# Two changes to a graph-network kernel: the dilation's compare goes from VectorE to GpSimd, and the layers' last batches are handled in smaller steps

## The chip, the cores and the metric

The kernel runs on one core of a Trainium2 chip. The metric is the device time of one execution in microseconds (us). A core has five engines that run their own instructions in order and wait for each other by semaphores: TensorE (in the profile PE, its weight loads PEld), VectorE (DVE), ScalarE (ACT), GpSimd (POOL) and SyncE (SP, which here only starts transfers).

## The reference, cut to what matters

There are B = 16 graphs of N = 1024 nodes with D = 128 features, and a dense weight matrix `adj` per graph. Two blocks follow each other.

Block 0 (`layer0` in the kernel) runs three times

```python
h = h @ W + b
nh = h / max(norm(h), EPS)
h = (adj * (nh @ nh.T)) @ h
```

on the normalised input and adds the result to `x`.

Block 1 first thins the adjacency out ("dilation"). Row by row, each row's present neighbours are counted; `rank` is the running count along the row, and every neighbour whose rank is a multiple of half the count (rounded up) is removed, with its mirror image, before the next row is looked at. With more than ten neighbours this removes the neighbour at half of the count, and the last one if the count is even. Rows with ten or fewer neighbours lose all. Then come three "sage" layers:

```python
out = (adj_d @ x / deg) @ Wr + x @ Wx + b
out = out / max(norm(out), NORM_EPS) * mask
h = batchnorm(relu(out))          # mean and variance over all 16 graphs
```

and the output is `concat(h1, h2, h3) @ Wl + bl`, masked and added to `x`. Because the batch norm needs the statistics of all sixteen graphs, a sage layer can't begin before the layer in front of it has ended for the last graph.

## The kernel before, in words

A graph is called a batch, P = 128, NCH = 8 chunks of 128 nodes, CPH = 4 chunks make a half. The program is written with a tile framework: the code gives the dataflow and its order, the framework's scheduler places each engine's instructions in an order of its own (with the code's order as the priority) and adds the semaphores. A tile's `tag` and `bufs` say how many copies of it exist; a new one has to wait until the last user of the oldest copy is done.

**Layer 0 and the dilation, together.** `layer0()` is a generator of units of TensorE work. Each block row of a batch takes a product of the normalised features (`pg`, L344), a multiplication with `adj` on VectorE (`ew`, L353 and L356), transposes (`gt`, L373) with a copy on ScalarE (L374), and sums (`po`, L384 and L398). `hS` (L321, GpSimd) holds the normalised features of a batch; the adjacency's transposed blocks are stored from GpSimd's queue (L262). `dilation()` is a second generator. The main loop takes a piece of the dilation, then as many units of layer 0 as a fixed share of estimated work allows, and so on, so that the two advance together.

The dilation goes over 16 blocks: eight row blocks `k` of 128 rows, each in two halves of BH = 8 batches. A block has three parts.

- `loads`: fetches `adj`, turns it into a 0/1 pattern (L587, L588) and multiplies the part left of the diagonal with what earlier row blocks kept (`kl`, read back from DRAM by a transposing transfer, and `patt`, L594).
- `rounds`: settles within the block which neighbours go, by iterating small steps between VectorE (`E` at L667 and a dozen operations on single columns) and TensorE (L673). It leaves `radius` and `shift`, so that a neighbour is to be removed exactly where |shift - rank| equals radius.
- `scans`: for each batch a running sum over 1024 columns on VectorE (`rank`, L740, three buffers), the absolute value of its distance from the shift on ScalarE (L749, in place), a comparison with the radius (`kp`, L760 on VectorE, two buffers), and a store of the result to DRAM from GpSimd's queue (`keep`, L761).

The comparison in question is

```python
nc.vector.tensor_scalar(kp, rank, radius[:, i : i + 1], None, ALU.not_equal)
nc.gpsimd.dma_start(keep_d[b][cols, :], kp)
```

A second form of the dilation (`exact=True`) stands in a branch that is taken only if the first found a row that it can't treat; with these inputs it doesn't run.

**The sage layers.** Per batch, `weighted` makes `hw` and `own` (`pw`, L860 to L862), `Sums.add` accumulates 64 blocks in PSUM (`agg`, L888), `weigh` divides by the degree and adds (`o`, L917). `norms(h)`, per half, squares four chunks on ScalarE (L933), takes the inverse root in three small steps (`ss`, `rn`, L154 to L157), multiplies with the mask (L937) and scales four chunks at once on GpSimd (L938). `keep(h)` transposes the half (`pt_r`, L165), applies relu on ScalarE into `hR` (L166) and takes statistics (L948). After the last batch `batchnorm` combines all statistics (L953 to L961) into a factor and an offset per feature. `normed` applies them to a batch with one ScalarE instruction (L1052).

In the second and third sage layer `start2(l, b)` is called while batch b - 1 is at its third block row. It normalises batch b's features of the layer before, begins its sums, and projects those same features with `wl` (`pp`, L1062) into `acc`: a copy for the first layer's features, an addition for the second's. In the third layer `residual(b)` multiplies `acc` with the squared mask and adds `x`. After the third layer a last loop over the batches normalises, projects and adds into `y`, which is stored.

Of the kernel before, what the change touches and what calls it, by code (L numbers as in the profile page):

```python
# [12 lines left out]
ALU = mybir.AluOpType  # L13
# [33 lines left out]
def tile_adj_preln_d2(  # L47
# [152 lines left out]
    with ExitStack() as actx:  # L200
# [362 lines left out]
        def dilate(k, half, exact):  # L563
# [161 lines left out]
            def scans():  # L725
# [9 lines left out]
                for i in range(BH + 1):  # L735
# [18 lines left out]
                    if exact:  # L754
                        nc.vector.tensor_scalar(
                            kp, rank, low[:, i : i + 1], radius[:, i : i + 1], ALU.max, ALU.not_equal
                        )
                        nc.vector.tensor_tensor(kp, kp, pt[:, 2:], ALU.is_ge)
                    else:
                        nc.vector.tensor_scalar(kp, rank, radius[:, i : i + 1], None, ALU.not_equal)  # L760
# [76 lines left out]
    with ExitStack() as bctx:  # L837
# [29 lines left out]
        class Sums:  # L867
# [58 lines left out]
            def norms(self, h):  # L926
# [4 lines left out]
                for c in range(CPH):  # L931
                    n = h * CPH + c
                    nc.scalar.activation(  # L933
                        self.own[:, n, :], self.o[:, n, :], AF.Square, accum_out=ss[:, c : c + 1]
                    )
                rn = inv_root(pool2, ss, nm)
                nc.vector.tensor_tensor(rn, rn, mf[:, b, hc], ALU.mult)  # L937
                nc.gpsimd.tensor_tensor(  # L938
                    self.o[:, hc, :], self.o[:, hc, :], rn.unsqueeze(2).to_broadcast([P, CPH, D]), ALU.mult
                )  # L940
# [24 lines left out]
        with kctx, ExitStack() as c1:  # L965
# [42 lines left out]
            def follow():  # L1008
                nonlocal last
                s, q, aT = behind.pop(0)  # L1010
                s.add(q, aT)
                if q == CPH + 1:
                    s.norms(0)
                if q == NCH - 1:
                    s.norms(1)
                    last = s
# [33 lines left out]
        def normed(l, b, ab):  # L1050
            hT = pool2.tile([P, NCH, P], F32, tag="hT2", name=f"hT2_{l}_{b}")
            nc.scalar.activation(  # L1052
                hT.rearrange("p c q -> p (c q)"), hR[:, b, :], AF.Identity, bias=ab[:, 1:2], scale=ab[:, 0:1]
            )
# [9 lines left out]

        def start2(l, b):
            hT = normed(l, b, ab)
            got = Sums(l, b, hT, CPH, 0, ps_a)
            for h, pp, a in project(l - 1, b, hT):
                if l == 1:
                    nc.scalar.activation(a, pp, AF.Copy)  # L1070
                else:
                    nc.vector.tensor_tensor(a, pp, a, ALU.add)
            return got
# [12 lines left out]
        for l in (1, 2):  # L1086
            last = None
            then = start2(l, 0)
            for b in range(B):
                now = then  # L1090
# [17 lines left out]
                now.norms(1)  # L1108
                last = now
            last.keep(1)  # L1110
            ab = batchnorm(l)

# [68 lines left out]
```

## Time and profile before

| | us |
|---|---|
| median of 3 runs | 2877.07 (2874.56 to 2882.93) |
| the profiled execution's own time | 2874.98 |
| its span in the profile | 2873.2 |
| TensorE busy | 2659.3 (93%) |
| VectorE busy | 1939.7 (68%) |
| ScalarE busy | 1426.0 (50%) |
| GpSimd busy | 473.7 (16%) |

The comparisons of L760 lie between 86.9 and 1565.8 us of the span, layer 0 ends near 1692, and the three sage layers end near 2150, 2490 and 2829 us. In the profile a group of instructions is given as line, engine, operation, output <- inputs by the program's names, shapes and count, then busy time in us and mean of one in ns, then the idle time of its engine just before them and what ended most of it. "x128" is a count. PEclk is TensorE's granted clock as a share of the full one. Matmuls are pipelined, so a busy TensorE isn't a TensorE at its peak. In a timeline the number in brackets is the engine's idle time before the instruction, in us.

### The profile page before, as it was taken

How to read it: one execution, taken by the hardware profiler on the slowest of the kernel's cores; microseconds unless marked ns; L12 is line 12 of the kernel's file. 1: busy time of each engine (PE TensorE's matmuls, PEld its weight loads, DVE VectorE, ACT ScalarE, POOL GpSimd, SP SyncE). 2: the span in 40 equal slices, each digit the busy share in tenths (PEclk: the TensorE clock that was granted, in tenths of full speed). 3: DMA queues.
4: the chain of work that ended last, by engine and by line, in shares of the span. 5: the costliest groups of instructions: out<-in, count | busy, mean ns of one | idle time of the engine just before them, and what ended most of it. 6: DMA issues, size and time to landing. Idle time of an engine off the chain costs nothing. (4 is left out here: it accounts for less than half of the span.)

```text
span 2873.2 us, 51953 instructions
## 1 busy us (share of the span) xinstructions
PE 2659.3 (93%) x18803; PEld 2199.0 (77%) x18803; DVE 1939.7 (68%) x4913; ACT 1426.0 (50%) x4100; POOL 473.7 (16%) x619
## 2 busy tenths in 40 slices
PE   6999998999999998989998998999989999899997
PEld 4666666666666666666676778898879999899996
DVE  3778778778878778789877467677762333356565
ACT  6767557557556556556455333333333433333334
POOL 3112112112011111112111012222220010010102
PEclk9999999999999999999999999999999999999998
DMA  9447247248366476286253249999985665577764
GB/s 287 130 139 236 77 155 236 86 137 247 87 186 178 99 199 191 80 257 191 55 190 115 75 168 380 379 401 401 397 333 191 202 213 202 183 236 229 237 230 134
DMA packets 382233, 585.22 MB, mean 204 GB/s; under 512 B 85200, under 2 KB 266448, under 8 KB 381968
## 3 DMA queue, kind: packets, MB, share of 16 engines
q1 hardware_dynamic: 343280, 425.28, 47.2%
q0 software_dynamic: 38688, 156.53, 14.5%
q8 instruction: 151, 2.47, 0.4%
q14 instruction: 114, 0.93, 0.1%
HBM read 403.44 MB, written 163.58 MB: 197 GB/s over the span
## 5 line engine op out<-in xcount | busy, mean ns | idle before, releaser
L888 PE MATMUL agg<-hw,aT 128*128 128x128 f32 (+1 forms) x6144 | 744.4, 277 | 8.2 <-DVE aT L985 7.3
L888 PEld LDWEIGHTS agg<-hw,aT 128*128 128x128 f32 x6144 | 713.6, 193 | 13.4 <-DVE aT L985 9.7
L344 PE MATMUL pg<-nhT 128*128 128x512 f32 (+3 forms) x1152 | 460.2, 502 | 69.5 <-DVE ew L356 65.5
L384 PE MATMUL po<-ew,hS 128*128 128x512 f32 (+3 forms) x1152 | 458.4, 501 | 8.7 <-ACT hTo L407 5.4
L356 DVE TENSOR_TENSOR ew<-pg,adjA 128x768 f32<-128x768 f32 (+3 forms) x528 | 423.2, 825 | 5.8 <-PE pg L344 5.7
L398 PEld LDWEIGHTS po<-ew,hS 128*128 128x128 f32 x2688 | 338.4, 193 | 40.3 <-issue 37.8
L398 PE MATMUL po<-ew,hS 128*128 128x128 f32 x2688 | 365.3, 277 | 1.2 <-ACT ew L374 1.2
L374 ACT ACTIVATE ew<-gt 128x512 f32<-128x512 f32 (+1 forms) x480 | 209.2, 465 | 247.8 <-PE gt L373 237.6
L344 PEld LDWEIGHTS pg<-nhT 128*128 128x128 f32 x1152 | 189.0, 194 | 164.8 <-issue 120.9
L740 DVE TENSOR_TENSOR_SCAN rank<-patt 128x1024 f16<-128x1024 f16 x128 | 295.0, 2316 | 0.9
L384 PEld LDWEIGHTS po<-ew,hS 128*128 128x128 f32 x1152 | 197.9, 195 | 100.8 <-issue 66.4
L373 PEld LDWEIGHTS gt<-ident,ew 128*128 128x128 f32 x1344 | 168.3, 143 | 100.2 <-issue 72.1
L353 DVE TENSOR_TENSOR ew<-pg,adjA 128x128 f32<-128x128 f32 x384 | 107.6, 280 | 184.9 <-PE pg L344 142.8
L938 POOL TENSOR_TENSOR o<-o,rn 128x512 f32<-128x512 f32 x96 | 111.4, 1160 | 646.6 <-DVE rn L937 627.7
L373 PE MATMUL gt<-ident,ew 128*128 128x128 f32 x1344 | 212.7, 276 | 4.9 <-PEq L822 2.4
L860 PE MATMUL pw<-wrx,hT 128*128 128x256 f32 x768 | 179.5, 388 | 10.5 <-ACT hT L1052 9.7
L862 DVE TENSOR_TENSOR own<-pw,bs 128x256 f32<-128x256 f32 x192 | 81.3, 424 | 156.9 <-ACT hw L861 156.8
L860 PEld LDWEIGHTS pw<-wrx,hT 128*128 128x128 f32 x768 | 145.0, 194 | 32.6 <-ACT hT L1052 10.5
L933 ACT ACTIVATE own<-o 128x128 f32<-128x128 f32 x384 | 114.4, 300 | 104.1 <-DVE o L917 104.0
L1003 ACT ACTIVATE aT<-pta 128x512 f32<-128x512 f32 (+3 forms) x160 | 71.1, 466 | 187.7 <-PE pta L1002 164.2
L749 ACT ACTIVATE rank<-rank,fin 128x1024 f16<-128x1024 f16 x128 | 146.7, 1151 | 30.8 <-DVE rank L740 30.2
L321 POOL TENSOR_TENSOR hS<-hN,rn 128x1024 f32<-128x1024 f32 x48 | 97.2, 2025 | 372.4 <-DVE rn L157 265.9
(165 smaller groups left out, 3910.5 us busy)
## 6 DMA issues: line engine op xcount, KB each, us to landing
an<-in_adj_dram SPq DMA_DIRECT2D x128, 512.0 KB, 4.4
keep<-kp POOLq DMA_DIRECT2D x128, 256.0 KB, 2.9
kb<-keep SPq DMA_DIRECT2D x128, 256.0 KB, 5.6
aT<-adT SPq DMA_DIRECT2D x32, 960.0 KB, 4.7
aT<-adT SPq DMA_DIRECT2D x32, 832.0 KB, 4.6
aT<-adT SPq DMA_DIRECT2D x32, 704.0 KB, 4.2
aT<-adT SPq DMA_DIRECT2D x32, 576.0 KB, 3.4
xb<-in_x_dram SPq DMA_DIRECT2D x31, 512.0 KB, 4.9
```

The lines of the kernel that those rows point to most:

```text
L344: nc.tensor.matmul(pg[:, :n, :].rearrange("p c q -> p (c q)"), lhsT=self.nhT[:, q * P : (q + 1) * P], rhs=self.nhT[:, (q + c) * P : (q + c ...
L356: nc.vector.tensor_tensor(both[0][:, :, off, :], pg[:, own:n, :].unsqueeze(1).to_broadcast([P, 2, n - own, P]), both[1][:, :, off, :], ALU ...
L373: nc.tensor.transpose(pt[:, i, :], ew[:, at + i, :], ident)
L374: nc.scalar.activation(ew[:, at : at + n, :], pt[:, :n, :], AF.Copy)
L384: nc.tensor.matmul(self.po[:, c * P : (c + n) * P], lhsT=self.hS[:, q, :], rhs=ew[:, c - q : c - q + n, :].rearrange("p c q -> p (c q)"), ...
L398: nc.tensor.matmul(self.po[:, q * P : (q + 1) * P], lhsT=self.hS[:, q + n, :], rhs=ew[:, NCH - 1 - q + n, :], start=False, stop=closes and ...
L740: nc.vector.tensor_tensor_scan(rank, pt[:, 1 : N + 1], pt[:, 2:], 0.0, ALU.add, ALU.add)
L749: nc.scalar.activation(rank, rank, AF.Abs, bias=shift[:, i : i + 1], scale=1.0 if exact else -1.0)
L860: nc.tensor.matmul(pw[:, i, :], lhsT=hT[:, 2 * h + i, :], rhs=wrx[:, l, :], start=True, stop=True)
L888: nc.tensor.matmul(self.place(c), lhsT=aT[:, blk, :], rhs=self.hw[:, source, :], start=source == 0 and c % self.ga == 0, stop=ends(c, source),
L933: nc.scalar.activation(self.own[:, n, :], self.o[:, n, :], AF.Square, accum_out=ss[:, c : c + 1])
L938: nc.gpsimd.tensor_tensor(self.o[:, hc, :], self.o[:, hc, :], rn.unsqueeze(2).to_broadcast([P, CPH, D]), ALU.mult)
```

## The change

There are four edits.

1. In the dilation, the comparison goes from VectorE to GpSimd, as one instruction with two steps (equal to the radius, then less than 0.5, which is 1 where it was not equal). The store follows it on GpSimd's queue as before.
2. `norms` has a form `soon`, used for the second half of each sage layer's last batch: two of four squares on VectorE, and the scaling as four instructions on VectorE instead of one on GpSimd.
3. `normed` treats batch 0 in four instructions of two chunks instead of one of eight.
4. In the second and third sage layer, the last batch's projection is taken out of `start2` and put between that batch's sums and its `keep(1)`. Its results are added to `acc` after `batchnorm` in the code; in the third layer, where `residual` has already scaled `acc`, they are multiplied with the squared mask on the way.

```diff
@@ -757,7 +757,8 @@
                         )
                         nc.vector.tensor_tensor(kp, kp, pt[:, 2:], ALU.is_ge)
                     else:
-                        nc.vector.tensor_scalar(kp, rank, radius[:, i : i + 1], None, ALU.not_equal)
+
+                        nc.gpsimd.tensor_scalar(kp, rank, radius[:, i : i + 1], 0.5, ALU.is_equal, ALU.is_lt)
                     nc.gpsimd.dma_start(keep_d[b][cols, :], kp)
                     yield False, 0.8
 
@@ -923,21 +924,29 @@
                         ALU.add,
                     )
 
-            def norms(self, h):
+            def norms(self, h, soon=False):
 
                 nm, b = f"{self.l}_{self.b}_{h}", self.b
                 hc = slice(h * CPH, (h + 1) * CPH)
                 ss = pool2.tile([P, CPH], F32, tag="in_ss", name=f"ss_{nm}")
                 for c in range(CPH):
-                    n = h * CPH + c
-                    nc.scalar.activation(
-                        self.own[:, n, :], self.o[:, n, :], AF.Square, accum_out=ss[:, c : c + 1]
-                    )
+                    o, sq = self.o[:, h * CPH + c, :], self.own[:, h * CPH + c, :]
+                    if soon and c >= CPH // 2:
+                        nc.vector.scalar_tensor_tensor(
+                            sq, o, 1.0, o, ALU.mult, ALU.mult, accum_out=ss[:, c : c + 1]
+                        )
+                    else:
+                        nc.scalar.activation(sq, o, AF.Square, accum_out=ss[:, c : c + 1])
                 rn = inv_root(pool2, ss, nm)
                 nc.vector.tensor_tensor(rn, rn, mf[:, b, hc], ALU.mult)
-                nc.gpsimd.tensor_tensor(
-                    self.o[:, hc, :], self.o[:, hc, :], rn.unsqueeze(2).to_broadcast([P, CPH, D]), ALU.mult
-                )
+                if soon:
+                    for c in range(CPH):
+                        o = self.o[:, h * CPH + c, :]
+                        nc.vector.tensor_scalar(o, o, rn[:, c : c + 1], None, ALU.mult)
+                else:
+                    nc.gpsimd.tensor_tensor(
+                        self.o[:, hc, :], self.o[:, hc, :], rn.unsqueeze(2).to_broadcast([P, CPH, D]), ALU.mult
+                    )
 
             def keep(self, h):
 
@@ -1012,7 +1021,7 @@
                 if q == CPH + 1:
                     s.norms(0)
                 if q == NCH - 1:
-                    s.norms(1)
+                    s.norms(1, soon=s.b == B - 1)
                     last = s
 
             then = ahead1
@@ -1049,9 +1058,16 @@
 
         def normed(l, b, ab):
             hT = pool2.tile([P, NCH, P], F32, tag="hT2", name=f"hT2_{l}_{b}")
-            nc.scalar.activation(
-                hT.rearrange("p c q -> p (c q)"), hR[:, b, :], AF.Identity, bias=ab[:, 1:2], scale=ab[:, 0:1]
-            )
+
+            n = NCH if b else 2
+            for c in range(0, NCH, n):
+                nc.scalar.activation(
+                    hT[:, c : c + n, :].rearrange("p c q -> p (c q)"),
+                    hR[:, b, c * P : (c + n) * P],
+                    AF.Identity,
+                    bias=ab[:, 1:2],
+                    scale=ab[:, 0:1],
+                )
             return hT
 
         def project(l, b, hT):
@@ -1062,15 +1078,22 @@
                     nc.tensor.matmul(pp[:, c, :], lhsT=hT[:, h * CPH + c, :], rhs=wl[:, l, :], start=True, stop=True)
                 yield h, pp, acc[:, b, h * CPH : (h + 1) * CPH, :]
 
+        def taken(l, pp, a):
+
+            if l == 0:
+                nc.scalar.activation(a, pp, AF.Copy)
+            else:
+                nc.vector.tensor_tensor(a, pp, a, ALU.add)
+
         def start2(l, b):
+
             hT = normed(l, b, ab)
             got = Sums(l, b, hT, CPH, 0, ps_a)
+            if b == B - 1:
+                return got, hT
             for h, pp, a in project(l - 1, b, hT):
-                if l == 1:
-                    nc.scalar.activation(a, pp, AF.Copy)
-                else:
-                    nc.vector.tensor_tensor(a, pp, a, ALU.add)
-            return got
+                taken(l - 1, pp, a)
+            return got, None
 
         def residual(b):
 
@@ -1087,7 +1110,7 @@
             last = None
             then = start2(l, 0)
             for b in range(B):
-                now = then
+                now, hT = then
                 for q in range(NCH):
                     aT = row_of(q, f"{l + 1}_{b}")
                     nc.sync.dma_start(aT, adT_d[b][q])
@@ -1105,10 +1128,22 @@
                         now.norms(0)
                     if q == NCH - 2 and b == B - 1:
                         now.keep(0)
-                now.norms(1)
+                now.norms(1, soon=b == B - 1)
                 last = now
+
+            late = list(project(l - 1, B - 1, hT))
             last.keep(1)
             ab = batchnorm(l)
+            for h, pp, a in late:
+                if l == 1:
+                    taken(0, pp, a)
+                    continue
+
+                for c in range(CPH):
+                    n = h * CPH + c
+                    nc.vector.scalar_tensor_tensor(
+                        a[:, c, :], pp[:, c, :], mf2[:, B - 1, n : n + 1], a[:, c, :], ALU.mult, ALU.add
+                    )
 
         for b in range(B):
             y = pool2.tile([P, NCH, D], F32, tag=("o", "own")[b % 2], name=f"y_{b}")
```

## The prediction

> **What bounds the kernel.** First the page's busy times, then a table of stages, then the waits of TensorE (PE) and VectorE (DVE) in the first stage, then the durations of the instructions concerned, last the timeline around a layer's end.
>
> ```profile
> PE 2659.3 (93%) x18803; PEld 2199.0 (77%) x18803; DVE 1939.7 (68%) x4913; ACT 1426.0 (50%) x4100; POOL 473.7 (16%) x619
> ```
>
> PE is busy nearly all the time; GpSimd (POOL) is nearly idle. The stages (stretch, then busy time with instruction count for each engine, granted PE clock, DMA share, GB/s):
>
> ```profile
> 100.00:1570.00 1470.00, 1356.03 (x8539) 989.68 (x8537) 1172.07 (x2782) 878.20 (x2350) 242.24 (x309) 0.99 0.52 155
> 1570.00:1692.00 122.00, 118.79 (x687) 86.67 (x685) 56.05 (x141) 38.13 (x114) 8.44 (x6) 1.00 0.19 64
> ...
> 2142.00:2156.00 14.00, 7.68 (x22) 5.80 (x23) 4.94 (x12) 4.88 (x9) 1.72 (x2) 0.51 0.39 141
> ...
> 2483.00:2494.00 11.00, 4.47 (x13) 3.48 (x14) 3.17 (x10) 3.68 (x6) 1.04 (x1) 0.53 0.01 2
> ...
> 2822.00:2835.00 13.00, 6.63 (x30) 6.24 (x31) 3.73 (x12) 4.90 (x9) 1.41 (x2) 0.50 0.00 0
> ```
>
> The dilation runs under layer 0 until 1567 us. There PE lacks only 114 of 1470 us, so no relief of DVE can give more than that. The last three rows are the ends of the three sage layers: PE is idle half the time and has half its clock. Who holds PE before 1692 us, and what DVE itself waits for (total us, times, longest):
>
> ```profile
> PE pg L344 <- DVE ew L356: 65.5, 52, 3.8
> ```
>
> ```profile
> DVE kp L760 <- ACT rank L749: 49.4, 40, 4.5
> ```
>
> All rows of that view in which DVE ended PE's wait sum to about 90 us. The compare that moves, its neighbours, and GpSimd's large instruction:
>
> ```profile
> L760 DVE TENSOR_SCALAR kp<-rank,fin 128x1024 f16<-128x1024 f16 x128 | 68.6, 547 | 49.9 <-ACT rank L749 49.4
> ```
>
> ```profile
> L740 DVE TENSOR_TENSOR_SCAN rank<-patt x128: 2231/2281/3983, 77.0 to 1553.2; 128x1024 f16<-128x1024 f16 x128
> ```
>
> ```profile
> L321 POOL TENSOR_TENSOR hS<-hN,rn x48: 1890/1892/3671, 33.8 to 1655.6; 128x1024 f32<-128x1024 f32 x48
> ```
>
> The second and third show min/median/max in ns. The maxima are one event seen twice: where scan and hS meet, one waits for the other's end.
>
> **Edit 1, the compare on GpSimd: what DVE gets.** DVE loses 68.6 us of work and its 49.4 us of waits for the absolute values: 118 us. How much of that was late for PE? I followed each of PE's 91 waits on DVE back along DVE to the last point where DVE itself waited for PE, and added up the compares and their waits in that stretch, at most the wait's own length: 32 of the 90 us. The rest stands behind scans and products alone. So 118 us of DVE are worth 32 us of PE, 0.27 each.
>
> **What GpSimd's compare costs.** No row shows a one-input GpSimd instruction of 1024 elements. From below: memsets take 0.11 us for 8 elements and 0.20 for 128, a slope that gives 0.9 us at 1024. From above: hS, two f32 inputs, 1.9 us. The 128-column affine select, which reads one input and compares, takes 0.30, nearer to the steep end: I take 1.4 us. 128 x 1.4 = 180 us, on an engine busy 242 us of 1470, so its load binds nothing. Two returns of cost do:
>
> *Port.* The 48 hS (91 us) made the DVE instructions that they overlapped 24 us longer than their medians, 8.4 of it on L760, which goes. Scans, patterns (L594) and the small columns of the rounds lost time, E (L667) reads the same way and is counted with them; the products (L356), which read PSUM, lost none. I set a GpSimd compare of 1.4 us at the end of each of the 128 absolute values, after any scan then running, and added what is left of it when the next such DVE instruction starts: 57 meet, 44 us (18 at 0.9, 76 at 1.9).
>
> *The new wait.* `rank` has three buffers, so scan i+3 must wait for compare i. That was the same engine; in the changed program nearly every scan carries a wait on GpSimd. What stands behind it on DVE are the products that PE waits for. In the timeline, scan i+3 starts a median 10.6 us after absolute value i ends, but 12 of 125 within 1.5 us and 25 within 3. With 1.4 us and GpSimd's instruction in front (hS, or the adjacency store) I count 24 waits, 26 us (16 at 0.9, 39 at 1.9). The store behind each compare and every adjacency store and hS after it move by as much; PE waits for hS 0.3 us in all, and keeps are read back a row block later, so these cost nothing while GpSimd has idle time.
>
> DVE's net: 118 - 44 - 26 = 48 us, times 0.27: **13 us gained**. At 0.9 us: 118 - 18 - 16 = 84, 23 us. At 1.9: 118 - 76 - 39 = 3, 1 us. With no return at all, 32.
>
> Two rules speak to this. The Trainium skill (GPSIMD Engine Reference, Engine selection) wants elementwise work on VectorE, since GpSimd is about half as fast with two inputs, yet near line rate with one; its section on elementwise cycle accounting gives 1.03 to 1.8 cycles per element at 1.2 GHz, an estimate of 0.9 to 1.5 us here, which would make the gain 23 to 11 us. The same skill (Advanced Engine Details and Errata, Mode Summary) says that GpSimd and two-port Vector instructions block each other, which is the rows' 3983 against 2281 and the part that speaks against the change.
>
> **Edits 2 to 4, the layers' ends.** One of them:
>
> ```profile
> 2483.28 0.16 DVE L937 TENSOR_TENSOR rn<-rn,mf 128x4 f32<-128x4 f32 x1
> 2483.59 1.04 POOL L938 TENSOR_TENSOR o<-o,rn 128x512 f32<-128x512 f32 x1 [4.33 <-DVE rn L937]
> ...
> 2484.68 1.11 PE L165 MATMUL pt_r<-ident,o 128*128 128x128 f32 x4 [4.49 <-POOL o L938]
> ...
> 2489.35 2.37 ACT L1052 ACTIVATE hT<-hR,bn_ab 128x1024 f32<-128x1024 f32 x2 [0.81 <-DVE bn_ab L961]
> ...
> 2490.64 5.16 PE L860 MATMUL pw<-wrx,hT 128*128 128x256 f32 x16 [4.85 <-ACT hT L1052]
> ```
>
> Everything here is one chain. In brackets: PE's idle time before.
>
> *Scaling in four on DVE.* From the end of rn (2483.44) to the end of the transposes (2485.79) takes 2.35 us. Four DVE steps cost 0.18 (L154, four elements) to 0.28 us (L353, 128 from PSUM): 0.9 together, and 0.3 for the last transpose, 1.2. Saved 1.15 (0.9 to 1.4), at the first layer 0.8, because its first half still runs on GpSimd just before: 3.1 us for three ends. This cover gone, a DVE busy elsewhere would be late; only residual columns (L1080, 0.3 to 0.4 each) are there.
>
> *Squares half on DVE.* Two of 0.34 + 0.08 us follow the weighing on DVE as late as ACT's last two: 0.
>
> *Normalisation of batch 0 in four.* PE starts after 256 columns (0.38 us, row L861) instead of 1024 (1.24, L1052): 0.85 x 3 = 2.6 us.
>
> *The last batch's projection after the layer.* 16 matmuls, 1.95 us, leave a stretch where PE has no idle time and go into the 4.49 us before the transposes: 2 x 1.95 = 3.9 us. Their evictions come back on the chain. In the second layer two ACT copies (0.60 us) stand between squares: 0.2. In the third, eight accumulations of 0.34 us on DVE replace two of 0.69 and stand between the steps of rn and around the statistics, four of them not under another wait: 1.2 us. Unmoved, the projection's PSUM buffers would hold up batch 0's; they are emptied before.
>
> Sum: 3.1 + 2.6 + 3.9 - 1.4 = **8 us gained**, 5 to 12. The upper end is the clock: it is 0.51, 0.53 and 0.50 in the three rows above, and L860's 16 matmuls took 5.16 us against 3.62 with the clock up. Should less idle time keep the clock, each end gives another 1.5.
>
> Total 13 + 8 = 21 us from the profiled execution's own 2874.98 (span 2873.2): 2854. It stands 2.1 us below the median of the runs, so I say 2855.
>
> **Rivals.** *Cancelled:* PE's waits come from scans (2.28 us each, 16 of 128 right behind another), not from compares, and port and slot return the rest; the first stage gains 0 to 3 and the layers' ends remain: about 2867. For it: only 32 of 90 us had a compare in reach. Against: the 49.4 us of waits.
>
> *Slower:* scan i+3 waits for GpSimd. By the counts above, DVE's balance is zero at 1.9 to 2.0 us for the compare. At 2.5 us the port returns about 115 and the slots about 58 (both counts carried on at their last step), DVE loses 55 and PE 15: 7 us slower with the layers' ends, 2884, and from there it decides. At 3 us they return 155 and 75, DVE loses 112 and PE 30: 2899. A compare that queues behind hS, for whose rn GpSimd waits 184 us in all, does the same at any length. For it: GpSimd is in order and its queue waits mostly on other engines; against: the median of 10.6 us of slack.
>
> *Also:* the scheduler places the whole program anew, with 19 triple scans in place of 17 over the whole program; 5 us either way.
>
> **How the numbers follow.** Forecast, 0.62: 2855, its own range 2836 to 2865. Cancelled, 0.20: 2862 to 2872, mostly within 0.3%. Slower, 0.18: 2884 to 2900, about 2892. About 0.3% (8.6 us) is what a measurement can tell from no change, so faster lies below 2868: 0.62 and a little of the cancelled case, 0.65; same 0.17; slower 0.18. For 8 in 10 the range runs from 2831 (32 us, or 23 with the clock kept) to 2886, into the slower case.
>
> **What would show it.** Right: L760's successor at 1.2 to 1.6 us on POOL, PE's wait for L356 near 50 us, a new wait of scans on POOL under 40, scans' mean at 2.5 to 2.7 us, PE's gap before the last transposes down from 4.49 to about 1.6, and before the projection from 4.85 to 4. Wrong: a compare above 2 us, scans waiting over 100 us in all, or a dilation that ends after 1567.

## The result, and the profile after

The changed kernel takes 3079.58 us (median of 4 runs, 3075.25 to 3084.31), against 2876.86 us for the kernel before on the same chip: a ratio of 1.0703, 95% interval 1.0686 to 1.0721. It is 203 us slower, where 2855 us had been forecast. The profiled execution has a span of 3077.5 us. One execution among the experiments below, with four rank buffers, took 5437.88 us, nearly twice the three others of its kernel, and its numbers are given without it.

First the page's busy times. Because the diff adds lines, the compare is now L761, its store L762, the scaling L945 and L947, the normalisation L1064.

```profile
PE 2733.1 (89%) x18803; PEld 2240.6 (73%) x18803; DVE 1927.4 (63%) x4815; ACT 1427.1 (46%) x4097; POOL 975.6 (32%) x744
```

GpSimd's busy time doubles, from 473.7 to 975.6 us. VectorE's falls by only 12 us though 68.6 us of compares are gone: edits 2 to 4 add 6 us (it is 1921.5 us with edit 1 alone), and the scans became 16 us longer in all, from 295.0 to 311.3 us. The same matmuls, 18803 of them, show 74 us more of busy time. With the last point goes a lower clock in the table of stages (engines' busy times, then granted clock, DMA share, GB/s):

```profile
100.00:1570.00 1470.00, 1248.99 (x7357) 901.28 (x7356) 1003.65 (x2313) 783.63 (x2083) 635.56 (x374) 0.93 0.47 139
```

In the same stretch TensorE got 7357 matmuls done instead of 8539, and its mean clock was 0.93 instead of 0.99. The first sage projection (`pw`) starts at 1903.9 us instead of 1694.6: 209 us are lost before it, and 5 us are gained behind it. So the whole loss lies where the dilation runs under layer 0. The groups of the page that answer to the ones shown of before:

```profile
L761 POOL TENSOR_SCALAR kp<-rank,fin 128x1024 f16<-128x1024 f16 x128 | 501.6, 3920 | 372.9 <-ACT rank L749 368.5
...
L740 DVE TENSOR_TENSOR_SCAN rank<-patt 128x1024 f16<-128x1024 f16 x128 | 311.3, 2440 | 206.3 <-POOL kp L761 205.9
```

The compare takes a mean of 3.92 us, seven times its 0.547 us on VectorE, and VectorE stands idle before its scans for 206 us until such a compare ends. That idle time was 0.9 us before:

```profile
L740 DVE TENSOR_TENSOR_SCAN rank<-patt 128x1024 f16<-128x1024 f16 x128 | 295.0, 2316 | 0.9
```

VectorE's waits and TensorE's after the change, each up to 1900 us (total, times, longest):

```profile
DVE rank L740 <- POOL kp L761: 205.9, 62, 8.8
```

```profile
PE pg L344 <- DVE ew L356: 141.5, 58, 8.8
```

The second stood at 65.5, 52, 3.8 before: hardly more waits, but far longer ones; the longest is 8.8 us in both views. One such wait in the timeline (start, duration, engine, instruction, idle time of its engine before it):

```profile
1182.44 0.29 DVE L353 TENSOR_TENSOR ew<-pg,adjA 128x128 f32<-128x128 f32 x1 [0.43 <-PE pg L344]
...
1184.82 1.15 ACT L749 ACTIVATE rank<-rank,fin 128x1024 f16<-128x1024 f16 x1
...
1186.08 3.70 POOL L761 TENSOR_SCALAR kp<-rank,fin 128x1024 f16<-128x1024 f16 x1 [2.60 <-ACT rank L749]
...
1189.82 2.29 DVE L740 TENSOR_TENSOR_SCAN rank<-patt 128x1024 f16<-128x1024 f16 x1 [7.09 <-POOL kp L761]
...
1192.03 0.27 DVE L353 TENSOR_TENSOR ew<-pg,adjA 128x128 f32<-128x128 f32 x1
...
1192.21 1.81 DVE L356 TENSOR_TENSOR ew<-pg,adjA 128x768 f32<-128x768 f32 x2
...
1193.30 1.19 PE L344 MATMUL pg<-nhT 128*128 128x256 f32 x2 [3.60 <-DVE ew L356]
```

VectorE reaches the scan at 1182.73, 2.1 us before the absolute value that frees its buffer has even begun. It waits 3.3 us for ScalarE and then 3.7 us for GpSimd. The products of layer 0 (L353, L356) stand behind the scan in VectorE's queue and start without a further wait once it is over, and TensorE's next `pg` waits for them. The view calls the whole 7.09 us a wait for GpSimd, since GpSimd came last. Split like this one, the 206 us of all 62 waits are about 25 us until the absolute value is there, 6 us until GpSimd begins its compare, and 172 us in which the compare runs.

Summed over TensorE's instructions up to the first sage projection, its idle time rises from 146 to 280 us; 110 of the 134 us are put down to VectorE and 28 to ScalarE. The other 75 of the 209 us are more busy time of the same matmuls, which the lower clock can account for: the trace has 16 stretches of half clock in this stage before (54.6 us) and 49 after (232 us). They all last 3.41 us or a multiple of it, and half of the added 178 us, 89 us, is the most that they can have cost. They follow gaps of TensorE: of its 53 gaps of over 2 us in this stage, 45 have a half-clock stretch beginning in them or within 3.5 us of their end (12 of 18 before). The Trainium skill (TensorE: Matmul & The Clock Gate, Part 1) says that an idle window of about 3.4 us halves the clock. The stretches here have that length, but in the 3.4 us in front of 24 of the 49 (14 of the 16 before) the trace shows no gap that long, only shorter ones, mostly of 2 to 3 us.

### The profile page after: what moved, and what is told of

It is laid out like the page before. It is cut to its first block, busy times and chain, and to the rows that moved or that the text cites. A ratio compares the mean times of both kernels' runs of the same rounds, so it can differ in the third digit from the quotient of the medians.

```text
span 3077.5 us, 51875 instructions
## 1 busy us (share of the span) xinstructions
PE 2733.1 (89%) x18803; PEld 2240.6 (73%) x18803; DVE 1927.4 (63%) x4815; ACT 1427.1 (46%) x4097; POOL 975.6 (32%) x744
## 5 line engine op out<-in xcount | busy, mean ns | idle before, releaser
L761 POOL TENSOR_SCALAR kp<-rank,fin 128x1024 f16<-128x1024 f16 x128 | 501.6, 3920 | 372.9 <-ACT rank L749 368.5
L344 PE MATMUL pg<-nhT 128*128 128x512 f32 (+3 forms) x1152 | 476.8, 516 | 154.9 <-DVE ew L356 141.5
L384 PE MATMUL po<-ew,hS 128*128 128x512 f32 (+3 forms) x1152 | 489.2, 531 | 12.8 <-ACT hTo L407 9.6
L740 DVE TENSOR_TENSOR_SCAN rank<-patt 128x1024 f16<-128x1024 f16 x128 | 311.3, 2440 | 206.3 <-POOL kp L761 205.9
L356 DVE TENSOR_TENSOR ew<-pg,adjA 128x768 f32<-128x768 f32 (+3 forms) x528 | 423.2, 826 | 4.2 <-PE pg L344 4.1
L398 PEld LDWEIGHTS po<-ew,hS 128*128 128x128 f32 x2688 | 347.8, 197 | 41.6 <-issue 39.9
L398 PE MATMUL po<-ew,hS 128*128 128x128 f32 x2688 | 372.6, 280 | 0.1
L947 POOL TENSOR_TENSOR o<-o,rn 128x512 f32<-128x512 f32 x93 | 108.4, 1166 | 638.7 <-DVE rn L941 611.7
L384 PEld LDWEIGHTS po<-ew,hS 128*128 128x128 f32 x1152 | 208.6, 205 | 115.1 <-issue 83.7
L373 PEld LDWEIGHTS gt<-ident,ew 128*128 128x128 f32 x1344 | 179.2, 151 | 112.8 <-issue 83.9
L353 DVE TENSOR_TENSOR ew<-pg,adjA 128x128 f32<-128x128 f32 x384 | 108.1, 282 | 217.1 <-PE pg L344 168.3
L373 PE MATMUL gt<-ident,ew 128*128 128x128 f32 x1344 | 224.8, 288 | 6.6 <-PEq L823 3.3
L587 ACT ACTIVATE patt<-an 128x1024 f16<-128x1024 f32 (+7 forms) x128 | 86.6, 681 | 208.6 <-DVE rank L740 159.5
```

The source lines that it names most:

```text
L344: nc.tensor.matmul(pg[:, :n, :].rearrange("p c q -> p (c q)"), lhsT=self.nhT[:, q * P : (q + 1) * P], rhs=self.nhT[:, (q + c) * P : (q + c ...
L356: nc.vector.tensor_tensor(both[0][:, :, off, :], pg[:, own:n, :].unsqueeze(1).to_broadcast([P, 2, n - own, P]), both[1][:, :, off, :], ALU ...
L373: nc.tensor.transpose(pt[:, i, :], ew[:, at + i, :], ident)
L384: nc.tensor.matmul(self.po[:, c * P : (c + n) * P], lhsT=self.hS[:, q, :], rhs=ew[:, c - q : c - q + n, :].rearrange("p c q -> p (c q)"), ...
L398: nc.tensor.matmul(self.po[:, q * P : (q + 1) * P], lhsT=self.hS[:, q + n, :], rhs=ew[:, NCH - 1 - q + n, :], start=False, stop=closes and ...
L740: nc.vector.tensor_tensor_scan(rank, pt[:, 1 : N + 1], pt[:, 2:], 0.0, ALU.add, ALU.add)
```

## The experiments

Ratios are against the kernel before, run on the same chip (2874.5 to 2878.1 us).

**The two parts of the change.** `ends_only` has edits 2 to 4, `compare_only` has edit 1.

> Only edits 2 to 4 (the layers' ends); the compare stays on VectorE. In the changed kernel the span after the first sage layer's first product is 4.9 us shorter than before (1173.7 against 1178.6). If the loss belongs to the compare alone, this kernel takes 2877 - 5 = 2872 us (2869 to 2875). If the new order of the whole program had a part in the loss, it would be above 2885.

> Only edit 1 (the compare on GpSimd); the layers' ends as before. If the whole loss is the compare's: 3080 + 5 = 3085 us, VectorE's waits for GpSimd near 206 us and the compare at 3.7 us. If the ends' edits and the compare had hurt each other: clearly below 3075.

Measured: `ends_only` 2870.36 us, 0.9975 (0.9961 to 0.9988). `compare_only` 3082.98 us, 1.0719 (1.0690 to 1.0747). Edit 1 alone has the whole loss, and the layers' ends are a small gain. `ends_only` is faster than both kernels, though by only a quarter of a percent than the one before.

**What GpSimd's forms cost.** The kernel before, with a few instructions on GpSimd added behind its end, three times each, and some again in f32, which this excerpt leaves out. The scheduler placed them among the last loop over the batches, so that other engines work beside some of them and stand still beside others.

```diff
+nc.gpsimd.tensor_scalar(m[1], m[0], col, 0.5, ALU.is_equal, ALU.is_lt)   # L1136
+nc.gpsimd.tensor_scalar(m[1], m[0], col, None, ALU.is_equal)             # L1137
+nc.gpsimd.tensor_scalar(m[1], m[0], 3.0, None, ALU.is_equal)             # L1138
+nc.gpsimd.tensor_scalar(m[1], m[0], 3.0, None, ALU.mult)                 # L1139
+nc.gpsimd.tensor_scalar(m[1], m[0], 3.0, 0.5, ALU.mult, ALU.add)         # L1140
+nc.gpsimd.tensor_tensor(m[1], m[0], m[0], ALU.mult)                      # L1141
+nc.gpsimd.tensor_copy(m[1], m[0])                                        # L1142
+nc.gpsimd.tensor_scalar(m[1][:, :512], m[0][:, :512], col, 0.5, ALU.is_equal, ALU.is_lt)  # L1143
```

> The kernel before, and at its end, where GpSimd has little else, three times each: the compare in its two-step form, in a one-step form with the radius as a column and as a constant, a multiplication with a constant, a multiplication and addition, a product of two tensors, a copy, the two-step compare over 512 columns, and forms with f32 in place of f16. If each step costs: one step takes about 1.9 us against 3.7. If the column operand costs: the constant form is much shorter. If f16 costs: the f32 forms are near 1.9 us. If it is a fixed cost: 512 columns take much more than 1.9 us. The copy, by the prediction's lower end, 0.9 us. The added work lengthens the kernel's end by some 60 us, which is of no interest.

GpSimd's groups in that stretch (busy us, mean ns, idle time before; L1148 is the form of L1136 in f32):

```profile
L1136 POOL TENSOR_SCALAR m<-m,m_col 128x1024 f16<-128x1024 f16 x3 | 11.1, 3716 | 0.1
...
L1148 POOL TENSOR_SCALAR m32g<-m,m_col 128x1024 f32<-128x1024 f32 x3 | 11.1, 3706 | 0.1
...
L1137 POOL TENSOR_SCALAR m<-m,m_col 128x1024 f16<-128x1024 f16 x3 | 8.5, 2848 | 0.3
L1139 POOL TENSOR_SCALAR m<-m 128x1024 f16<-128x1024 f16 x3 | 8.3, 2778 | 0.3
...
L1138 POOL TENSOR_SCALAR m<-m 128x1024 f16<-128x1024 f16 x3 | 8.3, 2769 | 0.3
L1143 POOL TENSOR_SCALAR m<-m,m_col 128x512 f16<-128x512 f16 x3 | 6.0, 2006 | 0.3
L1141 POOL TENSOR_TENSOR m<-m 128x1024 f16<-128x1024 f16 x3 | 5.7, 1893 | 0.2
...
L1140 POOL TENSOR_SCALAR m<-m 128x1024 f16<-128x1024 f16 x3 | 3.1, 1047 | 0.1
L1142 POOL COPY m<-m 128x1024 f16<-128x1024 f16 x3 | 3.1, 1038 | 0.2
```

Contention isn't what makes the change's form long: its three instances here took 3.714, 3.718 and 3.717 us, the second with VectorE idle all the time and the others with VectorE busy for 1.7 and 0.7 us of it. The median in the kernel is 3.71 us as well; only the mean there, 3.92 us, is 0.2 us above. Neither the comparison itself (a plain multiply takes as long, L1139), nor the column in place of a constant (L1137 against L1138), nor the second step as such explains it: multiply and add, two steps, takes 1.05 us. One step costs 2.8, two 3.7, and only certain forms come near one element per ns. A straight line through L1136 and L1143 has an estimate of 3.3 ns per column and 0.3 us fixed.

**The compare's length alone.** `cheap_op` puts the multiply-add in the compare's place, `one_compare` the one-step form, whose mask comes out inverted. Both have `compare_only`'s order of instructions on every engine, but for one small memset.

```diff
-nc.gpsimd.tensor_scalar(kp, rank, radius[:, i : i + 1], 0.5, ALU.is_equal, ALU.is_lt)
+nc.gpsimd.tensor_scalar(kp, rank, 0.0, 1.0, ALU.mult, ALU.add)                        # cheap_op
+nc.gpsimd.tensor_scalar(kp, rank, radius[:, i : i + 1], None, ALU.is_equal)           # one_compare
```

> Edit 1 alone, with GpSimd's compare put in place by a multiply and add with constants (the stored mask is all ones, and the test for stray blocks is held at zero so that the exact repeat does not run): 1.05 us in the run of GpSimd's forms, against 3.71 for the compare. The order of instructions on every engine is that of the kernel with edit 1 alone; only the length of this one operation changes. Theory (price: the prediction's sum holds, and the one wrong term was 1.4 us for an operation that takes 3.7): scans wait for GpSimd 15 to 30 us in all, the first sage projection starts at 1670 to 1690, 2855 to 2870 us. Rival (the wait itself: any GpSimd operation between absolute value and scan stops VectorE's queue often enough): waits over 80 us and more than 2900 us. The 320-column part at 1.56 us gave 2934, but it left VectorE all its own work.

> Edit 1 alone, with the one-step compare with the column on GpSimd (the mask comes out inverted, and the test for stray blocks is held at zero): 2.85 us in the run of forms. Same order of instructions again. Theory (price, and waits that grow faster than the length): scans wait 90 to 140 us, 2930 to 3000 us. Rival (a threshold on two-step forms, or waits in proportion to the length): waits 158 us = 206 x 2.85 / 3.71, about 3033 us.

VectorE's waits in `cheap_op`, then in `one_compare`:

```profile
DVE rank L740 <- POOL kp L760: 68.2, 36, 5.2
```

```profile
DVE rank L740 <- POOL kp L760: 157.3, 57, 8.4
```

**The compare left out.** `no_compare` stores a constant tile instead; `no_compare_bufs4` has a fourth rank buffer besides (and one buffer instead of two for `T`, `Z` and `E`, which are tiles of the dilation's `rounds`).

```diff
-kp = poold.tile([P, N], F16, tag="kp", name=f"kp{nk}_{i}")
-nc.vector.tensor_scalar(kp, rank, radius[:, i : i + 1], None, ALU.not_equal)
 nc.gpsimd.dma_start(keep_d[b][cols, :], kp)       # kp: one tile of ones, set at the start
```

> The compare is left out on every engine: a constant tile of ones is stored in its place, and the test for stray blocks is held at zero. VectorE loses the 68.6 us of compares and 49.4 us of waits, and nothing comes back. The prediction's conversion says 32 us: 2845 us. Rival (VectorE's relief is worth nothing to TensorE, since its waits come from scans and products): 2868 to 2877 us. Above 2877 would mean that the new order of instructions costs by itself.

> The compare left out on every engine as in the run without it (2887 us), with four rank buffers in place of three; T, Z and E have one buffer (which cost nothing in the control). There, scans waited 31.2 us for the absolute value three before, which is most of the 49.4 us that the compares had waited for it on VectorE. Theory (the prediction's gain came back as that wait): with a fourth buffer it is under 5 us and the time falls to 2845 to 2868 us. Rival (relief of VectorE is worth nothing to TensorE whatever it waits for: its wait for TensorE's products only grows, 142.8 to 173.2 us): 2875 to 2890 us.

VectorE's waits, first in the kernel before, then in `no_compare`, then with the fourth buffer:

```profile
DVE ew L353 <- PE pg L344: 142.8, 97, 4.5
```

```profile
DVE ew L353 <- PE pg L344: 173.2, 112, 6.3
...
DVE rank L742 <- ACT rank L751: 31.2, 24, 4.6
```

```profile
DVE ew L353 <- PE pg L344: 176.6, 110, 7.8
...
DVE rank L742 <- ACT rank L751: 7.8, 7, 3.6
```

The series, with three rank buffers (length is the median in the kernel):

| what frees a rank buffer | length, us | scans wait, us (times) | first `pw` at, us | half-clock stretches, whole run | ratio (interval) |
|---|---|---|---|---|---|
| compare on VectorE (before) | 0.48 | under 1 | 1694.6 | 22 | 1 |
| absolute value (`no_compare`) | 0 | 31.2 (24) | 1707.1 | 19 | 1.0028 (1.0009 to 1.0046) |
| `cheap_op` | 1.04 | 68.2 (36) | 1730.5 | 25 | 1.0138 (1.0099 to 1.0177) |
| `one_compare` | 2.85 | 157.3 (57) | 1835.8 | 42 | 1.0460 (1.0430 to 1.0490) |
| changed kernel, edits 2 to 4 too | 3.71 | 205.9 (62) | 1903.9 | 55 | 1.0703 (1.0686 to 1.0721) |

Three theories fall here. The first, that the forecast's sum was right but for one price, expected 2855 to 2870 us of `cheap_op`; it gave 2912.83. An operation below the forecast's 1.4 us still loses. The second, that the scans' waits grow faster than the compare's length, expected 90 to 140 us of waits and at most 3000 us of `one_compare`; it had 157.3 us, in proportion to the length as the rival said, and took 3011.12 us. The third, that VectorE's relief was eaten by the wait through the buffers, expected 2845 to 2868 us of `no_compare_bufs4`. It gave 2882.58 us, 1.0020 (1.0006 to 1.0033), just what its control `dve_bufs4` gives with the compares on VectorE. So the program without compares is no faster than the one with them: VectorE waits longer for TensorE's products, 173 and 177 us instead of 143. One rival stays open. `no_compare` took 2886.95 us, above both of its expected ranges, and by its own expectation a time above 2877 us means that the new order of instructions costs something. About a tenth of VectorE's instructions do stand elsewhere than before, and `no_compare_bufs4` differs as much from `dve_bufs4`. What the relief would be worth in an unchanged order was not measured.

Each us that the compare takes costs more than the one before. From `no_compare` (in another order of instructions) to `cheap_op` it is 22 us of stage per us, then 58, then 79. With edit 1 alone, in the same order as `cheap_op` and `one_compare`, the first `pw` is at 1905.3 us and the scans wait 208.7 us. So in one and the same order, about 170 of the 206 us that `compare_only` loses come with the length from 1.04 to 3.71 us. How the other 35 us of `cheap_op` divide between the operation itself and the new order was not settled.

**More rank buffers.** Edit 1 and the kernel before, with four and with six buffers; to make room, `T`, `Z` and `E` have one buffer each.

```diff
-ranks[i] = rank = poold.tile([P, N], F16, tag="rank", bufs=3, name=f"rank{nk}_{i}")
+ranks[i] = rank = poold.tile([P, N], F16, tag="rank", bufs=6, name=f"rank{nk}_{i}")   # or 4
```

> The compare on GpSimd, with six buffers for the ranks instead of three (the room comes from Z, E and T, which get one buffer instead of two). Theory 1, the wait: a scan waits for the compare three scans earlier and holds the products behind it; with six buffers that wait falls from 206 us to under 50, and the time to 2880 to 2920 us. Theory 2, the port: GpSimd's 502 us of compares keep VectorE's two-input instructions out; the wait falls, but the time stays above 3030 us. Theory 3, GpSimd's queue: stores and hS come late behind 3.7 us compares; the time stays above 3030 us and TensorE waits for hS or for nat.

> The control for compare_bufs6: the compare on VectorE, six buffers for the ranks, one for Z, E and T. If the single buffers cost nothing: 2865 to 2880 us, and the 90 us that compare_bufs6 (2967) still lies above the kernel before are GpSimd's. If they are what costs: near 2960 us, and the wait for the buffers explains the whole loss.

> Edit 1 alone with four rank buffers (T, Z and E with one). With three the scans waited 205.9 us for GpSimd, with six 28.4. Theory (the wait through the buffers is the larger part of the loss): one buffer more takes off over half of it, 60 to 100 us are left, 2950 to 3000 us. Rival (GpSimd's own length and port are the larger part): above 3020 us.

> The kernel before with four rank buffers (T, Z and E with one): the control for the other two. With six it lost 1.2%. Theory (scans are placed earlier in VectorE's order as buffers allow, ahead of products that TensorE waits for): between, 2880 to 2905 us. Rival (only the count of six did that): 2870 to 2880 us.

VectorE's waits for the compare on GpSimd with four buffers, then with six:

```profile
DVE rank L740 <- POOL kp L760: 123.1, 43, 8.2
```

```profile
DVE rank L740 <- POOL kp L760: 28.4, 12, 5.0
```

| rank buffers | compare on GpSimd | compare on VectorE | difference |
|---|---|---|---|
| 3 | 3082.98, 1.0719 | 2877.17, 1 | 7.2% |
| 4 | 3018.75, 1.0482 (1.0449 to 1.0516) | 2882.87, 1.0018 (1.0003 to 1.0034) | 4.6% |
| 6 | 2966.75, 1.0314 (1.0287 to 1.0342) | 2911.47, 1.0118 (1.0090 to 1.0147) | 1.9% |

The waits go from 209 over 123 to 28 us and the difference from 206 over 136 to 55 us, with the compare as long as ever (means of 3.94, 3.96 and 4.04 us). The wait through the buffers is the greater part of the loss. It is not all of it: with six buffers 28 us of waits were left, as the theory of the wait had said, but the time of 2966.75 us lies between that theory's 2920 and its rivals' 3030. One more buffer took off two fifths of the wait instead of the expected half, and its time lies just under the rival's bound of 3020 us. Six buffers cost 1.2% by themselves; VectorE's instructions then stand in another order, and which placement costs it was not settled.

**GpSimd's work without the wait.** `beside` leaves the compare on VectorE and runs the same compare on GpSimd on each result, into a tile that nobody reads. `single_bufs` is its control: one buffer for T, Z and E and nothing else.

```diff
 nc.vector.tensor_scalar(kp, rank, radius[:, i : i + 1], None, ALU.not_equal)   # kp with 4 buffers
+nc.gpsimd.tensor_scalar(scr, kp, radius[:, i : i + 1], 0.5, ALU.is_equal, ALU.is_lt)
 nc.gpsimd.dma_start(keep_d[b][cols, :], kp)
```

> The compare stays on VectorE; behind each, GpSimd does a compare of the same form that nobody reads (kp has four buffers, so that no scan waits for it; Z, E and T have one). This is GpSimd's work alone: its hold on the port and on its own queue, without the wait of the scans. Theory 1 (the wait is all): within 15 us of dve_bufs6. Theories 2 and 3 (port, queue): 50 to 100 us above dve_bufs6, with VectorE's two-input instructions longer, or TensorE waiting for nat, hS or late stores.

> The kernel before with one buffer in place of two for T, Z and E, three for the ranks as before; the order of instructions is that of the kernel before on every engine. It is the control for the unread compare beside VectorE's and for the six rank buffers. Theory (the single buffers cost what the control with six rank buffers lost): 2905 to 2915 us, so the unread compare costs about 15. Rival (the six buffers cost, by scans that run ahead of the products): 2877 us, and the unread compare costs about 48.

`beside` 2925.98 us, 1.0171 (1.0133 to 1.0209); `single_bufs` 2881.21 us, 1.0005 (0.9989 to 1.0022). So the unread compares cost about 48 us with no scan behind them. (`beside` is 14.5 us above `dve_bufs6`, but that kernel has another order of instructions; `single_bufs` has nearly the order of `beside`.) VectorE's compares there waited as long for their absolute values as before, 50.4 us against 49.4:

```profile
DVE kp L760 <- ACT rank L749: 28.5, 25, 3.3
DVE kp L760 <- issue: 21.9, 13, 4.4
```

The second row names no releaser, but each of its 13 waits ends 0.09 us after an absolute value does, and no buffer of `kp` was still in use. What grew is VectorE's own instructions: those that overlap GpSimd's are about 100 us longer than their medians, against 24 in the kernel before and 54 in the changed one. These 48 us are thus more likely too much than too little for contention in the changed kernel, and they are near the 55 us that are left with six buffers.

**Part of the compares.** `every_other` gives GpSimd every second compare, `part320` the first 320 columns of each.

```diff
+nc.gpsimd.tensor_scalar(kp[:, :320], rank[:, :320], radius[:, i : i + 1], 0.5, ALU.is_equal, ALU.is_lt)
+nc.vector.tensor_scalar(kp[:, 320:], rank[:, 320:], radius[:, i : i + 1], None, ALU.not_equal)
```

> Every other compare on GpSimd, the rest on VectorE, three buffers. Half of the dose: if each compare costs the same, 2877 + 103 = 2980 us. If it is a wait that needs several compares in a row (two in GpSimd's queue, each 3.7 us), clearly less than half: 2900 to 2940 us, with VectorE's wait for GpSimd under 70 us.

> The first 320 of 1024 columns of each compare on GpSimd, the rest on VectorE, three buffers. By the menu (2.0 us for 512 columns, 3.7 for 1024) GpSimd's part takes 1.37 us, which is the price that the prediction assumed. The prediction's counts at that price: 26 us of scans held and 44 us of VectorE lost to the port, against only 68.6 x 0.31 = 21 us of VectorE's work saved: 2877 + 0.27 x 49 = 2890 us. If the counts were too low also at that price: above 2915 us.

`every_other` 2922.27 us, 1.0159 (1.0121 to 1.0196): half of the compares, a quarter of the loss, as the scans' waits (54.9 us) say. `part320` 2933.99 us, 1.0199 (1.0163 to 1.0236), far above the 2890 expected and in its rival's range. Its groups:

```profile
L760 POOL TENSOR_SCALAR kp<-rank,fin 128x320 f16<-128x320 f16 x128 | 218.0, 1704 | 407.0 <-ACT rank L749 385.4 <-DVE ln_mv_l L141 8.8 <-DVE mid L663 5.5
...
L763 DVE TENSOR_SCALAR kp<-rank,fin 128x704 f16<-128x704 f16 x128 | 69.2, 550 | 58.5 <-ACT rank L749 56.1 <-DMA keep<-kp 0.9 <-POOL kp L760 0.6
```

VectorE's 704 columns took 69.2 us, against 68.6 for all 1024 before: the median fell from 482 to 404 ns, but the mean did not. 111 of the 128 now overlap one of GpSimd's parts; these took a mean of 0.563 us and the other 17 of 0.464. So VectorE gets no relief here, while its scans wait 37 us for GpSimd and its compares 56 us, not 49, for absolute values. GpSimd's part took 1.56 us at the median and 1.70 at the mean, not the expected 1.37. The run therefore says little on a whole compare of 1.6 us; `cheap_op` and `one_compare` stand on both sides of that length.

## Why the prediction was wrong, step by step

Three terms of the sum failed. GpSimd's compare was taken at 1.4 us and takes 3.71. The scans' new wait was counted at 26 us; it is 206 us, and 68 us even with an operation of 1.04 us. VectorE's relief was counted as 32 us of TensorE's time, and a program without any compare shows no gain.

**What bounds the kernel: held.** TensorE does. The stage under layer 0 is where edit 1 acts, and the layers' ends are separate.

**What GpSimd's compare costs: wrong.** 1.4 us were taken, between bounds of 0.9 and 1.9; the form takes 3.71. The bounds came from a memset's slope and a two-input product. Both rows measured true at 1024 columns (0.95 us for the memset in the run of forms, 1.89 for the product), but neither is an upper bound for another form: the one-input compare takes twice the two-input product. The page that was quoted, of the Trainium skill (GPSIMD Engine Reference, Elementwise — side-by-side cycle accounting), has 1.03 to 1.8 cycles per element, the 1.8 as a best case and so not as an upper bound; the runs show 4.4 at 1.2 GHz for this form (3.72 us for 1024), and 1.2 for the copy. Its section on engine selection speaks of near line rate with one input, which the copy bears out and the compare contradicts.

**What VectorE gets: wrong.** 118 us of relief were to be worth 32 us of TensorE. In `no_compare`, where GpSimd returns nothing but the order of instructions is another, TensorE's idle time put down to VectorE fell by 11 us (90.3 to 79.1), and that put down to ScalarE rose by 23 (28.8 to 52.1). The step that failed is the tracing of each wait back to the compares in front of it, as if everything else stayed in its place. The longer waits for `pg` and for ScalarE say that VectorE, where it comes earlier to its products, often finds them not ready; how much the new order adds to that is open.

Of the 49.4 us of waits for absolute values, which were counted as lost, 31.2 come back at the scans: with the compare out of VectorE's queue, the scan is the next to need what the compare had waited for. The rival "cancelled" had named this outcome for the first stage; the run without compares is its case.

**The new wait: the mechanism held, its size did not.** It was named, with its place and the three buffers: 26 us at 1.4 us of compare, 16 at 0.9, 39 at 1.9. Measured are 68.2 us at 1.04 and 205.9 at 3.71. Two things were wrong in the count. It paired absolute values and scans by their place in ScalarE's and VectorE's queues, but ScalarE takes many of them in another order. Paired each with its own, 32 of 125 scans of the kernel before start within 1.5 us of their absolute value's end and 48 within 3, not 12 and 25; the median stays, 10.9 us. And the count moved compares into the timeline of before, where a scan can't come before the absolute value of the buffer it takes, because the compare that waits for that value stands in front of it on VectorE. In the changed program VectorE is ready for 20 of 125 scans before that value is there, as in the timeline above, though the median slack is still 7.7 us. It is the short end of the distribution that decides, not the median.

**The port: too dear.** 44 us were counted at 1.4 us, and on the forecast's own slope some 190 to 210 at 3.7. By the same measure (VectorE instructions that overlap GpSimd's, beyond their medians) 23.6 us became 54.0, and nearly the same 43 to 44 us at 1.04 and at 2.85 us of compare. Why it grew no more wasn't tested; a VectorE that waits before its scans has fewer instructions to be met, which fits the 100 us of `beside`, where it doesn't wait. The two maxima that the prediction calls one event are two of a kind: the scan of 3.98 us began 0.3 us behind an hS of 2.13 us, and the hS of 3.67 us began 0.3 us behind a scan of 2.24 us. The one that begins second is the long one. The scans' mean, 2.44 us, is even below the 2.5 to 2.7 expected.

**The conversion 0.27: wrong on the way back.** It came from many short overlaps and was used for returned time too. A scan that waits holds up all products behind it for 3.3 us at the mean and up to 8.8, and the clock drops behind most of TensorE's long gaps, as shown above. From `no_compare` to the changed kernel the scans' waits grow by 175 us and the stage by 197: 1.1 us per us. With the right length, but the forecast's counts and 0.27, the sum would have been about 2920 us, by carrying on its slopes (118 us less 211 and 99, times 0.27, and 8 gained at the ends). These slopes are those of the prediction's prices for 2.5 and 3 us; its counts at 1.4 and 1.9 us, carried on at their step, give 146 and 68 us at 3 us in place of its 155 and 75, and about 2895 us in place of 2899. The rival "slower" was the right one in direction and place. It had its threshold at 1.9 to 2.0 us, while the series shows a loss at 1.04 us already, and its 2899 us at 3 us is far below the 3011 us measured at 2.85.

**The layers' ends: right.** Forecast 8 us, 5 to 12; `ends_only` gains 6.8 us by the medians. In its trace the three layers and the last loop take 2.7, 3.6, 1.7 and 0.4 us less, 8.4 in all, and the first stage 2.8 more. Second layer's end of the changed kernel, in the timeline:

```profile
2687.30 1.95 PE L1078 MATMUL pp<-wl,hT 128*128 128x128 f32 x16
...
2690.97 0.87 DVE L945 TENSOR_SCALAR o<-o,rn 128x128 f32<-128x128 f32 x4
2691.37 0.71 PEld L165 LDWEIGHTS pt_r<-ident,o 128*128 128x128 f32 x4 [2.31 <-ACT ss L155]
2691.40 1.03 PE L165 MATMUL pt_r<-ident,o 128*128 128x128 f32 x4 [2.15 <-DVE o L945]
...
2696.65 2.93 PE L861 MATMUL pw<-wrx,hT 128*128 128x256 f32 x6 [4.21 <-ACT hT L1064]
```

The projection's 1.95 us now fill the gap before the transposes: 4.49 us became 2.15 (about 1.6 had been forecast). The scaling in four took 0.87 us as worked out, but the transposes still took 1.03 us, not the last one's 0.3, so 0.85 us were saved where 1.15 had been counted. The gap before `pw` fell from 4.85 to 4.21 us, close to the 4 named. Half clock still came at each end, so the upper end of that range was rightly not taken.

**The marks that had been named** for being wrong were all met: a compare above 2 us (3.71), scans waiting over 100 us (206), a dilation that ends after 1567 (its last compare starts at 1776.5).

## What to carry to other kernels

Before an operation goes to GpSimd, measure that very form there, at its size: neighbouring forms of the same instruction differed by 3.5 times. Relief for an engine that has long waits for the bounding engine may be worth little. Leave the operation out altogether in one run: if that gains nothing, little can be hoped for from moving it, unless the order of instructions changed as well. When an operation leaves a queue, look for who waits next for what it had waited for, and count buffers against the new holder's time, since one stalled instruction in an in-order queue holds up everything behind it.

## What the runs showed of the hardware

- GpSimd's instructions on a column or constant fall into classes over 1024 columns: 1.04 to 1.05 us for copy and multiply-add, 2.77 to 2.85 for one step, 3.71 to 3.72 for two with a comparison, alike for f16 and f32 in the forms tried in both, and 1.89 for a product of two tensors. A single multiply costs 2.7 times a multiply-add.
- The loss grew faster than its cause: from `one_compare` to `compare_only`, in the same order of instructions, 0.86 us more of compare and 51 us more of waits became 70 us of stage, with half-clock stretches of the whole run up from 42 to 53.
- GpSimd's compares slow VectorE without any wait between the two: in `beside` VectorE's instructions that overlap GpSimd's are about 100 us longer than their medians, and the kernel 48 us longer.
